# Two attentions and an MLP in one kernel: VectorE's order at a slot's head, inverse sums by transfer, and the order around the last attention

## The chip, the cores and the metric

The kernel runs on 1 core of one Trainium2 chip. Its time is the device time of one launch in microseconds (us). Three runs of the kernel before took 950.59, 950.79 and 953.49 us; their median is 950.79 us.

## What is computed

The input is 16 samples of 256 tokens with 256 features (x), a context y of the same shape, and the weights; all is float32. A sample goes through three attentions of 16 heads (16 features each) and an MLP. Cut to what matters:

```python
x = rmsnorm(x + softmax(rmsnorm(x) Wq . rmsnorm(y) Wk) rmsnorm(y) Wv Wo)   # layer 0: cross attention
h = ln(x);  x = x + attn(q=rope(h wq), k=rope(h wk), v=h wv, causal) wo    # layer 1: self attention
h = ln(x);  x = x + attn(q=rope(h wq), k=rope(y wk), v=y wv) wo            # layer 2: cross attention
h = ln(x);  out = x + gelu(h fc1) fc2                                      # MLP, 256 -> 1024 -> 256
```

Softmax is taken without subtracting a maximum. The sum of the exponentials comes out of the values' matmul as a seventeenth column of ones, and a record of all sums (`seen`) is looked at at the end: if one is too large, a second version of the layers runs. With these inputs it doesn't.

## The kernel before

There are 48 attentions (16 samples, 3 layers). `ORDER` (L31) gives their order by layer; attention i is run in slot i of the loop from L862 on. The order of every engine's instructions is the order of the code, since the whole is under a manual schedule (L845): nothing is reordered, and an instruction that waits holds up all that follow on its engine. DMAs are issued by SyncE's queue (SP), also in this order.

An attention has heads in two halves t and keys in two halves kc. A slot has four blocks (n = 0 to 3); with the causal mask it has three. In each block TensorE does the scores of the block (`scores`, L476, into a pair of two-bank PSUM tiles, tag S), the values of the block before (`value`, L515, into a one-bank tile, tag A, of which there is only one), and one dense product (L294 or L307, into a tag d, three of them). ScalarE turns scores into exponentials (L487) into `pt`, and for the causal attention GpSimd zeroes the part above the diagonal (L494). The values of an attention's last block come in block 0 of the next slot.

Around slot i, other attentions are at other stages:
- attention i + 2: its statistics (`stats`: squares at L246 for layer 0, batch-norm statistics at L256 and L257 else), its normalization (`norm`, L263), its transposes (`turn`, L274), and for layer 0 the query's scales that go through memory (`send`, `receive`: rq, L368 to L379);
- attention i + 1: q, k and v products, with rotation on VectorE (L406 to L435) and the values' bias (L456);
- attention i - 1: its last values; the inverse of its sums (`invert`, L549);
- attention i - 2: the multiplication by the inverse (`divide`, L564) and the output product (`project`, L572);
- attention i - 3, if of layer 0: `finish` (L581).

The way of the sums: ScalarE copies the values out of PSUM (L529); a DMA takes the rows of sums to DRAM (`hop`, L530) and one back in a form with 128 partitions (`sums`, L539), while eight DMAs bring the values into `oT` (L544). `invert` takes the reciprocal on VectorE (L554), adds the sums to `seen` on GpSimd (L555), sends the inverses to DRAM (L556), and one DMA of 8 rows brings them to every sixteenth partition of `first` (L560). `divide` spreads each to 16 partitions by a shuffle on VectorE (L566, into `inv`) and multiplies (L570).

VectorE's order in block 0 of a slot is: finish (i - 3), stats (i + 2), divide (i - 2), norm (i + 2), then the rotation of q (i + 1). For a causal slot with nothing to finish, stats come ahead of the scores; with something to finish, norm comes in block 1.

The MLP takes two samples at a time (`Mlp`, eight of them) and does each of its two products as seven products of a fast scheme (`up` 1, 5, 6, 2, 7, 3, 4, L711, and `down` with the same numbers, L772), with `mix` and `sum_a` making the sums that the scheme needs on VectorE. A result in PSUM is copied by ScalarE (`keep_sum`) or added by VectorE (`add_sum`); ScalarE does the gelu (L707). The first MLP's statistics, normalization and transposes are placed in the last two slots (L932 to L940), and after them L942 to L952 interleave the last attention's end with the first MLP's upward products. From L953 on, MLP g's downward products follow MLP g + 1's upward ones.

Of the kernel before, what the change touches and what calls it, by code (L numbers as in the profile page):

```python
# [42 lines left out]
FIRST = [i // HD * HD for i in range(32)]  # L43
# [3 lines left out]
def xattn_kernel(  # L47
# [99 lines left out]
    firsts = []  # L147
    for i in range(2):
        first = ctile([P, KC, S], f"first_{i}")
        nc.gpsimd.memset(first, 0.0)  # L150
        firsts.append(first)
# [13 lines left out]
    for i in range(2):  # L165
        pads.append([ctile([P, 32], f"pad{i}_{j}") for j in range(2)])
        nc.gpsimd.memset(pads[i][0], 0.0)

    idle = dense_ps()
    for n in range(2):  # L170
        nc.tensor.matmul(
            idle, lhsT=ident, rhs=firsts[0].rearrange("p t s -> p (t s)"), start=True, stop=True
        )
# [141 lines left out]
    class Att:  # L315
# [189 lines left out]
        def value(self, t, kc):  # L505
# [15 lines left out]
            if final:  # L521
                if t == 0:
                    self.av_sb = work.tile([P, KC, 2, S], F32, tag="av", name="av")
                    self.sums = work.tile([P, 2, 2 * H], F32, tag="sums", name="sums")
                    self.oT = work.tile([P, KC, S], F32, tag="oT", name="oT")

                    self.hop = dram.tile([2, KC, 8, S], F32, tag="hop", name="hop")
                av = self.av_sb[:, t]
                nc.scalar.copy(av, self.av)  # L529
                nc.sync.dma_start(  # L530
                    out=self.hop[0, t].rearrange("(r i) q -> r (i q)", i=2),
                    in_=av[HD:P:32].rearrange("r i q -> r (i q)"),
                )
                if t == 1:

                    for n in range(8):
                        r, i = n // 2, n % 2
                        if n == 3:
                            nc.sync.dma_start(  # L539
                                out=self.sums[:, 0], in_=self.hop[0].rearrange(  # L540
                                    "t g (a b) -> (t g a) b", b=2 * H
                                ),
                            )
                        nc.sync.dma_start(  # L544
                            out=self.oT[32 * r + HD * i : 32 * r + HD * i + HD],
                            in_=self.av_sb[32 * r : 32 * r + HD, :, i],
                        )

        def invert(self):  # L549

            sums = self.sums
            if self.layer == 0:
                nc.vector.tensor_scalar(sums[:, 0], sums[:, 0], 1e-30, None, ALU.max)
            nc.vector.reciprocal(sums[:, 1], sums[:, 0])  # L554
            nc.gpsimd.tensor_tensor(seen, seen, sums, ALU.add)  # L555
# [3 lines left out]
            self.first = firsts[self.i % 2]  # L559
            nc.sync.dma_start(  # L560
                out=self.first[0:P:HD], in_=self.hop[1].rearrange("t g q -> g t q")
            )

        def divide(self):  # L564
            inv = work.tile([P, KC, S], F32, tag="inv", name="inv", bufs=1)
            nc.vector.stream_shuffle(  # L566
                inv.rearrange("p t s -> p (t s)"),
                self.first.rearrange("p t s -> p (t s)"), FIRST,
            )
            nc.vector.tensor_tensor(self.oT, self.oT, inv, ALU.mult)  # L570
# [67 lines left out]
    class Mlp:  # L638
        def __init__(self, g, pool):
            self.g, self.pool = g, pool  # L640
            self.xs = [rows_of(2 * g + i) for i in range(2)]
# [4 lines left out]
        def norm(self):  # L646
            self.xns = [ln_apply(x, *st, self.pool) for x, st in zip(self.xs, self.st)]
            for x in self.xs:
                add_bias(x, R_FC2)

        def turn(self):
            self.hT = self.pool.tile([P, KC, 2, S], F32, tag="qm", name="hT3")
            for i, xn in enumerate(self.xns):
# [7 lines left out]
                nc.scalar.copy(self.hT[:, :, i, :], ps.rearrange("p (k s) -> p k s", s=S))  # L661

        def mix(self):

            b = self.hT
            self.ts = self.pool.tile([P, 4, S], F32, tag="av", name="ts")
            t1, t2, t3, t4 = (self.ts[:, i] for i in range(4))
# [14 lines left out]
        def half(self, i, j):  # L682

            if i == 0:
# [17 lines left out]
        def gelu(self, i, j, banks=None):  # L702
# [7 lines left out]

        def up(self, n):  # L711
            b, ts = self.hT, self.ts
            if n == 1:
                self.a = {}
# [3 lines left out]
                self.keep_sum(0, 0, self.X)  # L718
            elif n == 5:
                self.Z = psS.tile([P, 2, 512], F32, tag="S", name="upZ")  # L720
                self.Z = [self.Z[:, i] for i in range(2)]
                self.up_product(5, self.Z, up_s[0], ts[:, 0], True)
                self.keep_sum(1, 1, self.Z)
            elif n == 6:
                self.up_product(6, self.X, up_s[1], ts[:, 1], False)
                self.keep_sum(1, 0, self.X)
            elif n == 2:
                w = [dense_ps() for _ in range(2)]
                self.up_product(2, w, up_a(0, 1), b[:, 1, 0], True)
                self.add_sum(0, 0, w)  # L730
                self.gelu(0, 0)
            elif n == 7:
                self.up_product(7, self.X, up_a(1, 0), ts[:, 2], False)
                self.add_sum(1, 1, self.X)
                self.gelu(1, 1)
            elif n == 3:
                self.up_product(3, self.Z, up_s[2], b[:, 1, 1], False)
                self.add_sum(1, 0, self.Z)
                self.gelu(1, 0)
            elif n == 4:  # L740
                self.up_product(4, self.X, up_a(1, 1), ts[:, 3], False)
                self.a[0, 1] = self.half(0, 1)
                self.gelu(0, 1, self.X)

        def sum_a(self, n):

            if n == 1:
                self.s = {1: self.half(1, 2), 2: self.half(1, 3), 3: self.a[1, 0]}
# [23 lines left out]
        def down(self, n):  # L772
# [20 lines left out]
            if n == 1:  # L793
# [3 lines left out]
                self.X = bank(psA, "A")  # L797
# [47 lines left out]
    with tc.manual_schedule():  # L845
# [16 lines left out]
        for i in range(N_ATT):  # L862
# [7 lines left out]
            finishing = i >= 3 and att(i - 3).layer == 0  # L870
            for n in range(len(a.blocks)):
# [8 lines left out]
                if n == 0:  # L880
                    if i == 0:
                        a.v()
                        do(1, "spread")
# [529 lines left out]
```

## Time and profile before

| | us |
|---|---|
| median of three runs | 950.79 |
| the profiled execution | 953.16 |
| its span on the core | 951.43 |
| TensorE busy in it | 936.1 |
| VectorE busy | 666.0 |
| ScalarE busy | 571.9 |
| GpSimd busy | 294.6 |

The profile is that of one execution. PE is TensorE, DVE VectorE, ACT ScalarE, POOL GpSimd, SPq SyncE's queue. A row of the timeline has its start and its length in us, the engine, the line of the kernel, the operation, output<-input, shape and count; what stands in square brackets is how long the engine was idle just before and what ended that. A row of the list of waits has who waited, for whom, and then the total in us, how often, and the longest. A group of matmuls is counted busy from its first to its last, also if one in its middle waits. Float32 matmuls appear as two instructions each.

### The profile page before, as it was taken

The page shows a single profiled execution, that of the slowest core. Times are in us where ns is not written, and L with a number is a line of the kernel's source. Part 1 is how long each engine was busy: PE and PEld are TensorE (multiplying, and loading weights), DVE is VectorE, ACT ScalarE, POOL GpSimd, SP SyncE. Part 2 cuts the span into 40 slices and gives each one's busy share as a digit, 9 for nine tenths or more (in the row PEclk, how much of TensorE's full clock was granted, in tenths as well). Part 3 has the DMA queues.
Part 4 walks back from the last instruction along what each step waited for, and adds up shares of the span by engine and source line. Part 5 has one row for each costly group of instructions (what it writes and reads, how often), then busy time and mean ns, then how long its engine had stood idle before and what let it go on. Part 6 is the DMA issues. An engine that isn't in the chain of part 4 may idle for free.

```text
span 951.4 us, 30022 instructions
## 1 busy us (share of the span) xinstructions
PE 936.1 (98%) x12374; PEld 551.6 (58%) x12374; DVE 666.0 (70%) x1483; ACT 571.9 (60%) x821; POOL 294.6 (31%) x502
## 2 busy tenths in 40 slices
PE   8999999999999999999999999999999899999997
PEld 4444455445454545455454445445445699999997
DVE  4347768877776797677866768787776776667653
ACT  4666666766666766666766676666676634444440
POOL 4213454334334344144242423334112211222200
PEclk9999999999999999999999999999999999999999
DMA  9531221202121122110222101010101000000001
GB/s 316 171 97 29 78 71 32 71 18 79 25 70 28 42 54 73 24 33 19 72 71 74 32 22 27 19 29 21 26 21 26 13 24 23 13 12 23 23 24 47
DMA packets 66089, 46.96 MB, mean 49 GB/s; under 512 B 25364, under 2 KB 65044, under 8 KB 65944
## 3 DMA queue, kind: packets, MB, share of 16 engines
q1 hardware_dynamic: 64712, 43.89, 16.8%
q8 instruction: 100, 1.64, 0.7%
q10 hardware_dynamic: 1232, 1.07, 0.4%
q14 instruction: 45, 0.37, 0.1%
HBM read 26.54 MB, written 5.79 MB: 34 GB/s over the span
## 4 chain that ended last, share of the span: by engine, by line
PE 88%; DVE 5%; DMA 3%; POOL 1%; ACT 1%; issue 1%; SPq 0%; DVEq 0%; POOLq 0%
PE S L476 18%; PE A L515 17%; PE d L294 16%; PE d L307 15%; PE A L762 6%; PE upX L676 6%; PE downZ L762 3%; PE upZ L676 3%; PE d L274 2%; PE d L762 2%; PE d L676 1%; DMA hop<-av 1%; DVE a L410 1%; PE d L657 1%; DVE u L410 1%
## 5 line engine op out<-in xcount | busy, mean ns | idle before, releaser
L487 ACT ACTIVATE pt<-S 128x1024 f32<-128x1024 f32 x224 | 217.4, 1022 | 114.3 <-PE S L476 114.3
L476 PE MATMUL S<-qm,kT 32*128 32x512 f32 (+1 forms) x1536 | 202.9, 600 | 2.1 <-DVE kT L435 1.0
L515 PE MATMUL A<-pt,va 128*32 128x256 f32 (+1 forms) x3072 | 193.0, 367 | 1.3 <-POOL pt L494 0.8
L515 PEld LDWEIGHTS A<-pt,va 128*32 128x32 f32 x3072 | 80.5, 109 | 158.5 <-issue 95.4
L487 ACT ACTIVATE pt<-S,sy 128x1024 f32<-128x1024 f32 x128 | 135.7, 1111 | 46.1 <-PE S L476 44.0
L555 POOL TENSOR_TENSOR seen<-seen,sums 128x64 f32<-128x64 f32 x48 | 15.4, 320 | 280.4 <-DVE sums L554 185.8
L476 PEld LDWEIGHTS S<-qm,kT 32*128 32x128 f32 x1536 | 62.4, 183 | 68.5 <-issue 25.4
L494 POOL TENSOR_SCALAR_AFFINE_SELECT pt<-pt 128x512 f32<-128x512 f32 x128 | 88.5, 713 | 27.4 <-ACT pt L487 27.3
L283 POOL TENSOR_TENSOR cur<-cur,bias 128x512 f32<-128x512 f32 x48 | 65.3, 1365 | 58.9 <-DVE xn L263 58.9
L402 ACT ACTIVATE a<-d,qk_bias 128x256 f32<-128x256 f32 x128 | 53.8, 471 | 38.5 <-PE d L294 33.4
L294 PE MATMUL d<-hT,sa 128*32 128x256 f32 x1024 | 63.1, 379 | 0.0
L238 POOL TENSOR_SCALAR r_ln<-bmv 128x2 f32<-128x2 f32 x48 | 12.6, 261 | 153.3 <-DVE bmv L257 152.6
L529 ACT COPY av<-A 128x512 f32<-128x512 f32 x96 | 56.6, 590 | 3.5 <-PE A L515 3.2
L410 DVE TENSOR_TENSOR u<-u,turn 128x512 f32<-128x512 f32 x64 | 53.5, 836 | 0.0
L410 DVE TENSOR_TENSOR a<-a,turn 128x512 f32<-128x512 f32 x64 | 50.2, 784 | 2.2
L263 DVE TENSOR_SCALAR xn<-cur,bmv,r_ln 128x256 f32<-128x256 f32 x96 | 51.1, 579 | 0.8 <-POOL r_ln L239 0.6
L707 ACT ACTIVATE g<-g,fb 128x256 f32<-128x256 f32 x96 | 40.9, 497 | 15.4 <-DVE g L700 15.4
L579 DVE TENSOR_TENSOR cur<-d,cur 128x512 f32<-128x512 f32 x32 | 21.7, 679 | 38.8 <-PE d L307 38.7
L406 DVE STREAM_SHUFFLE u<-a 128x512 f32<-128x512 f32 x64 | 47.7, 746 | 0.0
L294 PEld LDWEIGHTS d<-hT,sa 128*32 128x32 f32 x1024 | 34.3, 110 | 22.1
L695 ACT COPY g<-upX 128x512 f32<-128x512 f32 x32 | 17.2, 589 | 46.8 <-issue 39.0
L757 DVE TENSOR_TENSOR g<-g,g 128x512 f32<-128x512 f32 x64 | 40.7, 681 | 0.0
(142 smaller groups left out, 1568.1 us busy)
## 6 DMA issues: line engine op xcount, KB each, us to landing
oT<-av SPq DMA_DIRECT2D x384, 32.0 KB
cur<-in_x SPq DMA_DIRECT2D x16, 256.0 KB
xT<-in_xt SPq DMA_DIRECT2D x16, 256.0 KB
yT<-in_yt SPq DMA_DIRECT2D x16, 256.0 KB
y<-in_y SPq DMA_DIRECT2D x16, 256.0 KB
out<-res SPq DMA_DIRECT2D x15, 256.0 KB
fc<-in_fc SPq DMA_DIRECT2D x2, 1024.0 KB
rq<-rq_hop SPq DMA_DIRECT2D x14, 128.0 KB
```

The costliest lines, as they stand in the source:

```text
L283: nc.gpsimd.tensor_tensor(t, t, bias_sb[:, row : row + D].unsqueeze(1).to_broadcast([P, NC, D]), ALU.add)
L294: nc.tensor.matmul(ps[j : j + 32, t * S : (t + 1) * S], lhsT=w[:, k, at + t * P + j : at + t * P + j + 32], rhs=src[:, k, :], start=(k == ...
L307: nc.tensor.matmul(ps[j : j + 32, c * D : (c + 1) * D], lhsT=src[:, k, c * P + j : c * P + j + 32], rhs=w[:, k, at : at + D], start=(k == ...
L402: nc.scalar.activation(a[:, t], ps[:, t], AF.Identity, bias=bias[:, t : t + 1])
L410: nc.vector.tensor_tensor(t, t, table.unsqueeze(1).to_broadcast([P, KC, S]), ALU.mult)
L476: nc.tensor.matmul(ps[:, j, 2 * m * u : 2 * m * (u + 1)] .rearrange("p (i s) -> p i s", i=2), lhsT=self.kT[r, t, kc * P : (kc + 1) * P], r ...
L487: nc.scalar.activation(pt[:, :, :w], ps[:, :, :w], AF.Exp, scale=scale)
L494: nc.gpsimd.affine_select(out=diag, in_=diag, compare_op=ALU.is_ge, fill=0.0, base=0, pattern=[[0, 2], [0, 2], [1, P]], channel_multiplier=-1,
L515: nc.tensor.matmul(self.av[32 * r : 32 * r + 32, i, q0:S], lhsT=self.va[:, kc, 8 * t + 2 * r + i, :], rhs=pts[r // 2][:, r % 2, i * m : (i ...
L529: nc.scalar.copy(av, self.av)
L676: nc.tensor.matmul(banks[c // 2][:, (c % 2) * S : (c % 2 + 1) * S], lhsT=a[:, c * P : (c + 1) * P], rhs=b, start=(first and c % 2 == 0), s ...
L762: nc.tensor.matmul(ps[:, c, :], lhsT=a[f // 2][:, f % 2, c * P : (c + 1) * P], rhs=b[:, f, :], start=(first and c == 0 and f == 0), stop=True,
```

## The change

Six things are changed:

1. The copy of attention i - 1's last values is split off (`take`, `end`) and done by VectorE in block 0 of slot i, after the statistics, unless these belong to the sample that `finish` has just written (`follows`); then it stands ahead of finish. Norm (i + 2) now precedes divide (i - 2). The first half's copy stays on ScalarE.
2. In place of the 8-row DMA and the shuffle, two DMAs read each inverse row 16 times and write all 128 partitions of `inv`, which now has two buffers. The two `first` tiles go; a tile of zeros takes their place in the two matmuls at the start.
3. The addition to `seen` moves from `invert` to `divide`, a slot later.
4. `invert` precedes `v` in the block before the last.
5. Around the last attention: the first MLP's statistics and normalization move to slots 45 and 46, the second's to 46 and 47; their transposes, the output product of attention 45 and the first MLP's product 2 are placed between the last slot's blocks; VectorE copies both transposes; `up` accepts products 1 and 2 in either order, and the gelu's order is written out by hand (`ups`).
6. For the last MLP, three of the four `sum_a` are done during the MLP before it, into other buffers, and the PSUM bank of its downward products comes from the tag S instead of A.

The diff, cut to its core:

```diff
-                av = self.av_sb[:, t]
-                nc.scalar.copy(av, self.av)
+                self.take(t, nc.scalar.copy)
+        def take(self, t, copy):
+            av = self.av_sb[:, t]
+            copy(av, self.av)
+            nc.sync.dma_start(out=self.hop[0, t]..., in_=av[HD:P:32]...)
+        def end(self, copy=nc.vector.tensor_copy):
+            self.take(1, copy)
+            for n in range(8):
...
             nc.vector.reciprocal(sums[:, 1], sums[:, 0])
-            nc.gpsimd.tensor_tensor(seen, seen, sums, ALU.add)
             nc.sync.dma_start(out=self.hop[1]..., in_=sums[:, 1])
-            self.first = firsts[self.i % 2]
-            nc.sync.dma_start(
-                out=self.first[0:P:HD], in_=self.hop[1].rearrange("t g q -> g t q")
-            )
+            self.inv = work.tile([P, KC, S], F32, tag="inv", name="inv")
+            for t in range(KC):
+                nc.sync.dma_start(
+                    out=self.inv[:, t],
+                    in_=self.hop[1, t].unsqueeze(1).to_broadcast([8, HD, S]),
+                )
         def divide(self):
-            inv = work.tile([P, KC, S], F32, tag="inv", name="inv", bufs=1)
-            nc.vector.stream_shuffle(inv..., self.first..., FIRST)
-            nc.vector.tensor_tensor(self.oT, self.oT, inv, ALU.mult)
+            nc.gpsimd.tensor_tensor(seen, seen, self.sums, ALU.add)
+            nc.vector.tensor_tensor(self.oT, self.oT, self.inv, ALU.mult)
...
+            follows = (
+                finishing and i + 2 < N_ATT
+                and att(i + 2).layer == 1 and att(i + 2).b == att(i - 3).b
+            )
...
                 if n == 0:
+                    if not follows and (finishing or not a.causal):
+                        do(i + 2, "stats")
+                    do(i - 1, "end")
                     do(i - 3, "finish")
-                    if finishing or not a.causal:
+                    if follows:
                         do(i + 2, "stats")
-                    do(i - 2, "divide")
                     if not finishing:
                         do(i + 2, "norm")
+                    if i == N_ATT - 3:
+                        mlps[0].stats()
+                    if i == N_ATT - 2:
+                        mlps[0].norm()
+                    do(i - 2, "divide")
+                    if i == N_ATT - 1:
+                        mlps[0].turn(nc.vector.tensor_copy)
+                        mlps[0].keep()
                     do(i + 1, "q")
                 elif n == 1:
...
+                    if i == N_ATT - 1:
+                        do(i - 2, "project")
+                        mlps[1].norm()
                 if n == final - 1:
+                    do(i - 1, "invert")
                     do(i + 1, "v")
-                    do(i - 1, "invert")
                     do(i + 2, "send")
+                    if i == N_ATT - 2:
+                        mlps[1].stats()
+                    if i == N_ATT - 1:
+                        mlps[0].up(2)
+                        mlps[0].mix("hT")
                 if n == final:
-                    do(i - 2, "project")
+                    if i == N_ATT - 1:
+                        mlps[1].turn(nc.vector.tensor_copy)
+                    else:
+                        do(i - 2, "project")
...
         last.values(-1)
+        last.end(nc.scalar.copy)
+        mlps[0].up(1)
         do(N_ATT - 2, "divide")
-        for n in (1, 5, 6, 2):
-            mlps[0].up(n)
+        mlps[0].ups(5, 6, (0, 0))
         do(N_ATT - 2, "project")
+        mlps[1].mix()
+        mlps[1].keep()
         last.invert()
-        for n in (7, 3, 4):
-            mlps[0].up(n)
-        mlps[1].turn()
-        mlps[1].mix()
+        mlps[0].ups(7, (1, 1), 3, 4, (0, 1), (1, 0))
...
+            if g == 0:
+                ahead.ups(2, 1)
...
+            final = g == B // 2 - 2
+            if final:
+                ahead.sum_a(1, ("qm", "av"))
             this.down(5)
+            if final:
+                ahead.sum_a(2)
...
-                self.X = bank(psA, "A")
+                if last:
+                    self.X = psS.tile([P, 2, 512], F32, tag="S", name="downX")
+                    self.X = self.X[:, 0, : NC * H2].rearrange("p (c d) -> p c d", d=H2)
+                else:
+                    self.X = bank(psA, "A")
```

In `ups` a tuple stands for the gelu of that quarter, a number for a product.

## The prediction

> **What bounds the kernel now.** I read the page's busy times first, then TensorE's own timeline from end to end, taking the distance from the start of one group of matmuls to the next, and last the list of waits.
>
> ```profile
> span 951.4 us, 30022 instructions
> ...
> PE 936.1 (98%) x12374; PEld 551.6 (58%) x12374; DVE 666.0 (70%) x1483; ACT 571.9 (60%) x821; POOL 294.6 (31%) x502
> ...
> PEclk9999999999999999999999999999999999999999
> ```
>
> TensorE is the bound at a full granted clock, and the change gives it the same matmuls; only their order near the end differs. So nothing is gained from shorter work on VectorE, ScalarE or GpSimd as such. What can be gained is time in which TensorE stands still or crawls, and 951.4 - 936.1 = 15.3 us understates it, since a group that waits in its middle counts as busy. I therefore use start-to-start distances. Undisturbed, scores to values take 1.07 us, values to a dense product 0.88, a dense product to the next scores 1.84: 3.80 a block. By that pace a slot without causal mask lasts 15.19 us (0.59 more with a transpose, 0.44 more after a causal slot), a causal slot 13.30. Most of the 47 slots before the last one have these lengths to 0.05 us. The excess lies in four places.
>
> (1) Slots. Over their own nominal length are slot 5 by 0.62, slot 6 by 0.98, 22 by 0.10, 29 by 1.00, 34 by 0.29, 39 by 0.48, 40 by 1.08, 41 by 0.83, 43 by 0.26: 5.6 us together. Slots 40 and 41 show both kinds:
>
> ```profile
> 625.83 0.66 PE L274 MATMUL d<-ident,xn 128*128 128x128 f32 x4
> 626.65 0.69 DVE L435 TENSOR_TENSOR kT<-a,u 128x512 f32<-128x512 f32 x1
> 627.49 1.14 PE L476 MATMUL S<-qm,kT 32*128 32x512 f32 x8 [1.01 <-DVE kT L435]
> 627.86 0.34 DVE L554 RECIPROCAL sums<-sums 128x32 f32<-128x32 f32 x1
> 628.29 0.32 POOL L555 TENSOR_TENSOR seen<-seen,sums 128x64 f32<-128x64 f32 x1 [5.77 <-DVE sums L554]
> 628.56 2.13 PE L515 MATMUL A<-pt,va 128*32 128x128 f32 x30
> 628.56 1.23 POOL L494 TENSOR_SCALAR_AFFINE_SELECT pt<-pt 128x512 f32<-128x512 f32 x2
> 630.52 0.39 PE L515 MATMUL A<-pt,va 128*32 128x256 f32 x2
> ```
>
> VectorE was late with the keys, so the scores began 1.0 us late. And GpSimd had stood still until the reciprocal, because the record of sums (L555) is ahead of the causal mask (L494) in its queue; the last two of 32 value matmuls came 0.6 us late. The list of waits gives the size of that block and of VectorE's own at a slot's head:
>
> ```profile
> POOL seen L555 <- DVE sums L554: 185.8, 34, 9.7
> ...
> DVE inv L566 <- DMA first<-hop: 34.7, 21, 3.6
> ```
>
> (2) The last attention and the first MLP, 721.1 to 767.1:
>
> ```profile
> 722.17 1.07 PE L515 MATMUL A<-pt,va 128*32 128x256 f32 x16
> 723.41 2.04 PE L476 MATMUL S<-qm,kT 32*128 32x512 f32 x8 [0.17 <-ACT pt L487]
> 725.38 1.07 PE L515 MATMUL A<-pt,va 128*32 128x256 f32 x16
> ...
> 739.68 1.89 PE L676 MATMUL d<-hT,fc 128*128 128x256 f32 x8
> 742.86 1.93 PE L307 MATMUL d<-cao,oT 128*32 128x256 f32 x32 [1.29 <-issue]
> ...
> 750.01 1.04 PE L657 MATMUL d<-ident,xn 128*128 128x128 f32 x8
> 752.88 1.99 PE L676 MATMUL upX<-hT,fc 128*128 128x256 f32 x8 [1.84 <-ACT hT L661]
> ```
>
> With nothing to project between blocks, scores overtake the exponentials: 0.24 + 0.90 (1.97 instead of 1.07) + 0.26. The projection at 742.86 comes 1.36 late (3.18 against 1.82), because its input was multiplied only at 741.6 to 742.8. The upward product at 752.88 comes 1.85 late (2.87 against 1.02), because ScalarE copies the transposed input behind eleven activations. Sum 4.6 us.
>
> (3) The entry to the last MLP:
>
> ```profile
> 930.97 1.95 PE L762 MATMUL A<-down_t,g 128*128 128x128 f32 x16
> 933.53 2.02 PE L762 MATMUL A<-fc,g 128*128 128x128 f32 x16 [0.61 <-DVE res L779]
> ```
>
> 2.56 instead of 1.78, as both groups use the one bank A; then 0.21 and 0.10 while VectorE does six sums at once. 1.1 us. (4) The first 30 us and the tail after the last VectorE operation at 947.0: about 6 us that no edit touches.
>
> **The change, part by part.**
>
> *Record of sums moved from invert to divide.* The 48 additions of 320 ns stay, but now stand at a slot's head, where their input is a slot old. The mask behind them no longer waits for a reciprocal. This covers slots 6, 22, 29, 34, 39, 41, 43: 3.9 us. What is late next is the exponential that the mask reads, and that is on time.
>
> *Head of a slot.* Statistics, copy of the last values, finish, norm, divide stand in this order, so VectorE works where it waited for the inverse. In slot 40 it sat idle 3.2 us until 617.64, then did shuffle, multiply and norm and reached the query's shuffle at 620.01. Now norm goes first (values end at 615.1, copy to 615.8, norm to 616.9) and only the multiply waits. The inverse must then be there by about 619 for the stall of 1.0 to go.
>
> *Copy of the values on VectorE.* 47 copies leave ScalarE (590 ns each; nothing waits for that there). VectorE's nearest row, 128x512 with one input from PSUM (L579), has 679 ns: 47 x 0.68 = 32 us more, against 48 x (745 + 14) ns = 36 us of shuffle and mask load less. Even. The bounds are 0.59 and 0.69; both end even. The copy waits for TensorE, and behind it stand finish, norm, divide and the query's evacuation. Values end about 2.0 us into the slot, the copy 2.9, and the next values need the bank at 4.87: 2 us of cover. It is about 1 us earlier than ScalarE's, which came behind two exponentials (288.03 in the slot that begins at 284.70), and so are the sums behind it.
>
> *Repeated inverse by transfer.* One DMA of 8 rows becomes two that write 128 partitions with 1 KB each. SyncE pays one more issue of 0.64 us per slot; in its queue the query scales (rq) and the next sample's loads stand behind that. The small DMA's data came 1.93 us after its issue (615.71 to 617.64). Packets cost 0.168 x 16 x 951.4 / 64712 = 40 ns at 678 bytes, so an estimated 60 ns at 1 KB; 256 packets over 16 engines are 1.0 us, so 2.9 us after the first issue. The Trainium skill (DMA: Bandwidth & Descriptors, "Why a DMA increments its semaphore by 16 and not by 1") speaks against that: the number of engines is the largest up to 16 that divides the slowest dimension of both patterns, and here the source begins with 8 heads, so 8 engines and 1.9 us: 3.8 us after issue. No row here tells the two apart. I take 3.8. Against 1.93 + 0.76 for transfer and shuffle this is 1.1 us later; the reciprocal, now ahead of the values' bias addition (680 ns), starts 0.7 earlier. In most slots TensorE doesn't feel it: the product reads oT ten microseconds after the head, and keys have 1.2 to 7 us of margin (end of the keys' last addition to the scores that read them). Keys with less than 0.8 us are those of slots 5, 22, 29, 39, 41, 43. I leave slot 5, where the stall is the late rq, unrecovered, count half of slot 40's and charge 0.9 us for new waits. Slots: 3.9 + 0.5 - 0.9 = 3.5, bounds 5.6 and -1.
>
> *Filled last attention.* The same groups in the order scores, values, transposes / scores, values, projection / scores, values, product 2 / scores, values, transposes / values, products. A filler takes 1.02 to 1.87, so scores begin 3.1 us or more after the last ones and find their bank free. Inputs: the first MLP's rows are normalized a slot earlier (2.3 us of VectorE where it idled 3.1 us at 707.6); transposes are copied by VectorE (4 x 0.68), so none waits behind activations; attention 46's inverse has all of slot 47. The last values may wait 0.3 for the exponential, and products 6 and 7 follow VectorE closely. 4.6 - 0.5 = 4.1 us.
>
> *Last MLP.* The first bank comes from the S pair, which products no longer need; six sums of 0.64 move into the MLP before, where VectorE was 12.65 of 23.8 us busy. 1.1 us. The idle start matmuls read another zero tile: nothing.
>
> Sum: 4.1 + 1.1 + 3.5 = 8.7. The profiled execution took 953.16, of which the span is 951.43; after, 942.7 of span and 944.5 for the execution. The median of the runs shown is 2.4 lower than that execution. If those 2.4 lie outside the span, the median after is 942.1; if they are slot stalls the other runs did not have, it stays 944.5. I put 943.0.
>
> **Rivals.**
>
> *All of it goes* (0.12): no new wait at all, 4.6 + 1.1 + 5.6 = 11.3, 939.5. For it: most slots have over 1.2 us margin.
>
> *The slots' stalls change place* (0.20): the mask runs on time, but an inverse or rq that is 1 us later delays six tight slots by as much as is won, and the last attention gives 3 of its 4.6: about 4, 946.8. For it: the 8 engines, and six margins under 0.8 us. Against it: the norm now precedes the wait.
>
> *Slower* (0.05): the copy holds the values' only PSUM bank. Where two samples' squares stand ahead of it (13 slots), VectorE enters late and TensorE waits for the bank. The 2 us cover must be overrun by 8.7 / 13 = 0.67 us in each to cancel everything; by 0.95 us it is 954. Against it: in eight of these slots the squares end by 2.4 us after the head, when the copy's input has only just come.
>
> The forecast itself has 0.63.
>
> **How the numbers follow.** Low end: 939.5 less the 0.2 by which runs differ, 939.3. High end: just past the second rival, 947.6. Measurement can tell about 0.3%, 2.9 us, from no change. Faster by that means under 947.9: the first case, all of it, and most of the second rival, 0.89. Same 0.06, slower 0.05.
>
> **What would show it.** Right: no wait of GpSimd's record for a reciprocal; value groups after causal slots unbroken; the first downward product of the first MLP 4 us or more earlier after slot 47's head than 46.0; 1.78 between the last two MLPs; slots 29, 39 and 41 at 16.22. Wrong: waits of TensorE for the copy of the values, VectorE waiting longer for the inverse than 34.7 us with keys late behind it, or product 6 waiting for VectorE.

## The result, and the profile after

The changed kernel takes 946.16 us (median of six runs, 945.57 to 947.51); the kernel before, run beside it, 952.05 (six runs, 950.59 to 953.49). The ratio is 0.9942, with a 95% interval of 0.9929 to 0.9954: 5.9 us faster. The profiled execution took 945.63 us, 943.8 of it span.

From the page of the changed kernel, the span and the first busy times:

```profile
span 943.8 us, 29943 instructions
...
PE 931.4 (99%) x12374; PEld 550.1 (58%) x12374; DVE 656.8 (70%) x1438; ACT 546.8 (58%) x770; POOL 297.6 (32%) x501
```

The same 12374 matmuls, 7.6 us less span. Start-to-start distances of TensorE's groups, as in the prediction, say where they went. "Excess" is what slots last beyond their undisturbed length (13.30 and 15.19 us with the prediction's additions; the 0.59 for a transpose is now left out in slots that transpose nothing).

| profiled execution, us | before | after | difference |
|---|---|---|---|
| start of slot 0 | 10.89 | 11.06 | +0.17 |
| excess of slots 0 to 3 | 2.50 | 2.70 | +0.20 |
| excess of slots 4 to 9 | 2.19 | 4.30 | +2.11 |
| excess of slots 10 to 46 | 5.35 | 0.07 | -5.28 |
| head of slot 47 to first downward product | 46.04 | 42.31 | -3.73 |
| first to last downward product | 177.48 | 176.34 | -1.14 |
| rest | 6.8 | 6.8 | 0 |

So the last attention, the last MLP and all late slots gave what they had, and some of it was lost again in slots 4 to 9. TensorE's timeline of the changed kernel around slot 41's head:

```profile
625.82 1.14 PE L472 MATMUL S<-qm,kT 32*128 32x512 f32 x8
...
626.89 1.51 PE L511 MATMUL A<-pt,va 128*32 128x128 f32 x32
```

The scores wait for no keys (1.01 before), and the 32 value matmuls of the causal slot are one unbroken group of 1.51 (2.13 and a rest of 0.39 before). The last attention and the entry to the last MLP, in the same view:

```profile
720.37 1.09 PE L657 MATMUL d<-ident,xn 128*128 128x128 f32 x8
721.40 1.26 PE L472 MATMUL S<-qm,kT 32*128 32x512 f32 x8
...
737.08 1.89 PE L681 MATMUL upX<-ts,up_s 128*128 128x256 f32 x8
738.90 1.93 PE L303 MATMUL d<-cao,oT 128*32 128x256 f32 x32
...
926.23 1.95 PE L779 MATMUL downX<-fc,g 128*128 128x128 f32 x16
928.01 1.95 PE L779 MATMUL downZ<-down_t,g 128*128 128x128 f32 x16
```

A filler stands between blocks; the projection follows the upward product by 1.82 (3.18 before); and the groups of the last MLP are 1.78 apart (2.56 before). The list of waits shows what is new:

```profile
DVE qm L417 <- DMA rq<-rq_hop: 36.1, 12, 4.8
...
POOL seen L566 <- DVE sums L554: 19.0, 2, 12.5
...
PE A L511 <- DVE av L528: 2.5, 2, 1.6
```

GpSimd's record waited for a reciprocal 34 times before; the two waits that are left stand in and behind the last slot. VectorE's waits for the inverse are down to 8.0 us in the same list (34.7 before). But TensorE now waits for VectorE's copy of the values, in slots 4 and 6: the mechanism of the prediction's "slower" rival. And VectorE waits longer for the queries' scales rq: 36.1 us, 23.8 before.

### The profile page after: what moved, and what is told of

Read it like the earlier page. It is cut to its first block, busy times and chain, and to the rows that moved or that the text cites. A ratio compares the mean times of both kernels' runs of the same rounds, so it can differ in the third digit from the quotient of the medians.

```text
span 943.8 us, 29943 instructions
## 1 busy us (share of the span) xinstructions
PE 931.4 (99%) x12374; PEld 550.1 (58%) x12374; DVE 656.8 (70%) x1438; ACT 546.8 (58%) x770; POOL 297.6 (32%) x501
## 3 DMA queue, kind: packets, MB, share of 16 engines
q8 instruction: 100, 1.64, 0.7%
q10 hardware_dynamic: 1232, 1.07, 0.4%
## 4 chain that ended last, share of the span: by engine, by line
PE 87%; DMA 6%; DVE 4%; SPq 2%; issue 1%; POOL 0%; ACT 0%; ACTq 0%; DVEq 0%
PE S L472 17%; PE A L511 16%; PE d L303 15%; PE d L290 15%; PE upX L681 6%; PE A L779 5%; PE downZ L779 3%; PE upZ L681 3%; PE d L270 2%; PE d L779 2%; PE d L681 1%; DMA hop<-sums 1%; DMA sums<-hop 1%; DMA hop<-av 1%; DMA rq_hop<-pad 1%; PE d L657 1%
## 5 line engine op out<-in xcount | busy, mean ns | idle before, releaser
L511 PE MATMUL A<-pt,va 128*32 128x256 f32 (+1 forms) x3072 | 188.9, 367 | 2.5 <-DVE av L528 2.5
L567 DVE TENSOR_TENSOR oT<-oT,inv 128x512 f32<-128x512 f32 x48 | 41.5, 864 | 30.5 <-DMA hop<-av 8.5
L290 PE MATMUL d<-hT,sa 128*32 128x256 f32 x1024 | 61.2, 379 | 0.0
L406 DVE TENSOR_TENSOR a<-a,turn 128x512 f32<-128x512 f32 x64 | 48.1, 752 | 2.2
L417 DVE SCALAR_TENSOR_TENSOR qm<-d,vec,rq 128x512 f32<-128x512 f32 x32 | 22.5, 746 | 38.8 <-DMA rq<-rq_hop 36.1
L406 DVE TENSOR_TENSOR u<-u,turn 128x512 f32<-128x512 f32 x64 | 49.2, 768 | 0.0
L528 DVE COPY av<-A 128x512 f32<-128x512 f32 x47 | 32.2, 684 | 21.8 <-PE A L511 21.8
L234 POOL TENSOR_SCALAR r_o<-ms_o 128x2 f32<-128x2 f32 x16 | 5.1, 322 | 128.9 <-DVE sq L242 117.0
```

What stands on the lines that cost most here:

```text
L290: nc.tensor.matmul(ps[j : j + 32, t * S : (t + 1) * S], lhsT=w[:, k, at + t * P + j : at + t * P + j + 32], rhs=src[:, k, :], start=(k == ...
L406: nc.vector.tensor_tensor(t, t, table.unsqueeze(1).to_broadcast([P, KC, S]), ALU.mult)
L511: nc.tensor.matmul(self.av[32 * r : 32 * r + 32, i, q0:S], lhsT=self.va[:, kc, 8 * t + 2 * r + i, :], rhs=pts[r // 2][:, r % 2, i * m : (i ...
```

## The experiments

The times of before beside these runs were 952.22, 951.98 and 952.15 us. The table has the excess from each kernel's one profiled execution, which for e1, e2 and e3 took 1.9 to 3.6 us more than the median, so that their columns are at the upper end. The last column, the time that the inverses of slot 40 take out to memory, is explained under code loading, below.

| kernel | median us | ratio, 95% interval | slots 4-9 | slots 10-46 | head 47 to down | slot 40: excess (way of the inverses to memory) |
|---|---|---|---|---|---|---|
| before | 952.05 | 1 | 2.19 | 5.35 | 46.04 | 1.08 (3.07) |
| after | 946.16 | 0.9929-0.9954 | 4.30 | 0.07 | 42.31 | 0.01 (1.46) |
| e1_v_first | 948.10 | 0.9951-0.9977 | 4.80 | 3.48 | 42.31 | 1.65 (3.45) |
| e2_copy_first | 949.88 | 0.9965-0.9990 | 6.99 | 5.22 | 42.31 | 1.65 (2.99) |
| e3_both | 953.30 | 1.0005-1.0026 | 6.63 | 7.59 | 42.49 | 1.66 (3.09) |
| e4_record | 945.18 | 0.9917-0.9952 | 2.58 | 1.32 | 42.32 | 0.00 (1.46) |
| e10_record_only | 949.43 | 0.9959-0.9979 | 0.21 | 1.56 | 46.45 | 1.45 (2.61) |
| e5_shuffle | 942.50 | 0.9885-0.9918 | 0.00 | 0.18 | 42.76 | 0.05 (1.42) |
| e11_end_act | 947.87 | 0.9928-0.9961 | 6.01 | 0.12 | 42.31 | 0.00 (1.47) |
| f1_spare_rows | 944.63 | 0.9904-0.9935 | 4.24 | 0.12 | 42.77 | 0.00 (1.48) |
| f2_spare_repeated | 945.22 | 0.9912-0.9947 | 3.15 | 0.06 | 42.77 | 0.00 (1.46) |
| f3_shuffle_but_last | 942.82 | 0.9887-0.9920 | 1.12 | 0.20 | 42.32 | 0.05 (1.42) |
| e6_old_last | 947.92 | 0.9945-0.9975 | 3.00 | 0.02 | 44.87 | 0.00 (1.46) |

**First theory: VectorE's order at the head is what makes slots 4 and 6 wait.** In the changed kernel, VectorE stood at the inverse's sums until 75.48 us with the values' bias behind them; then came four squares, then the copy, 1.59 us late for TensorE. Three kernels change that order, one takes the record's move back.

e1: the values' bias ahead of the inverse, as before.

```diff
-                    do(i - 1, "invert")
                     do(i + 1, "v")
+                    do(i - 1, "invert")
```

> The changed kernel with one thing put back: the values' bias (v) stands ahead of invert again. Theory (VectorE's own queue makes the new waits of slots 4 to 7): in slot 3 the bias and all behind it no longer wait 3.3 us for the sums, so the copy of slot 4 is about 0.9 us earlier and its wait of 1.6 us shrinks to about 0.7; the same in slot 6; the reciprocals come 0.7 us later, which the late slots bear. About 945.2 us against 946.2 for the changed kernel. Rival (the larger inverse transfers make those waits): no change, 946.2.

e2: the copy always ahead of the statistics.

```diff
-                    if not follows and (finishing or not a.causal):
-                        do(i + 2, "stats")
                     do(i - 1, "end")
+                    if not follows and (finishing or not a.causal):
+                        do(i + 2, "stats")
```

> The changed kernel with the copy of the last values ahead of the statistics in every slot. Theory: the waits of TensorE for that copy in slots 4 and 6 (1.6 and 0.9 us) go, while the squares come up to 0.7 us later, which can lengthen the two waits for the query scales by as much: 944.2 us, between 943.5 and 945.5. Rival (transfers): the waits stay, 946.2. Second rival: statistics behind the copy make norm and keys late in the slots with 0.4 us of margin, 947 or more.

e3: both.

> Both edits together: bias ahead of invert, copy ahead of the statistics. Theory: the two gains overlap, since both free the same copy; 943.9 us, at most 0.5 below the copy alone. Rival (transfers): 946.2.

All three are slower than the changed kernel, by 1.9 (the intervals just touch), 3.7 and 7.1 us, and the more of the cure, the worse. Slot 4 of e1 loses 0.56 in place of 1.67, as the theory said, but slots 35 and 40 now stall (1.49 and 1.65). In e2, with the copy first, no matmul of slots 4 and 6 waits for the copy any more, and yet they lose 2.19 and 3.17: in slot 6 a product waits 1.88 us for the values' bias. The theory fell. Slot 40 of e1, VectorE, TensorE and SyncE's queue:

```profile
614.72 0.33 SPq L555 DMA_DIRECT2D hop<-sums  x1
...
618.17 1.30 SPq L560 DMA_DIRECT2D inv<-hop  x2
...
621.79 0.86 DVE L567 TENSOR_TENSOR oT<-oT,inv 128x512 f32<-128x512 f32 x1 [2.92 <-DMA inv<-hop]
...
630.28 1.14 PE L472 MATMUL S<-qm,kT 32*128 32x512 f32 x8 [1.58 <-DVE kT L431]
```

The inverses' way out to memory took 3.45 us (614.72 to 618.17, where the next transfer may be issued), against 1.46 in the changed kernel; the multiplication, the rotation behind it and the keys are late in turn.

e4: the record of sums put back where it was, all else as changed.

```diff
             nc.vector.reciprocal(sums[:, 1], sums[:, 0])
+            nc.gpsimd.tensor_tensor(seen, seen, sums, ALU.add)
...
         def divide(self):
-            nc.gpsimd.tensor_tensor(seen, seen, self.sums, ALU.add)
```

> The changed kernel with the record of sums back in invert, right behind the reciprocal. Theory: the causal mask waits for reciprocals again, and the slots after a causal one (29, 34, 39, 41, 43) lose what they had lost before less the 0.7 us by which the reciprocal is now earlier: 2.5 us in all, 948.7. Rival (the gain of those slots comes from VectorE's new order alone): no change, 946.2.

945.18: the time is no longer than with the move. Two slots, 6 and 34, show the old block, and no other does; slot 34:

```profile
521.98 0.32 POOL L555 TENSOR_TENSOR seen<-seen,sums 128x64 f32<-128x64 f32 x1 [5.58 <-DVE sums L554]
...
523.09 1.43 PE L511 MATMUL A<-pt,va 128*32 128x256 f32 x14 [0.55 <-POOL pt L490]
```

They lose 1.40 and 1.33 us in this execution. In slots 29, 39, 41 and 43 the reciprocal is 0.4 to 1.1 us earlier against the slot's head than in the kernel before, and there before the mask is due. That comes from its place ahead of the bias: in e1, where the bias is first again, it comes 0.2 to 0.4 us behind the head, about as late as before the change.

e10 is the counterpart: the kernel before, with the record moved and nothing else.

```diff
-            nc.gpsimd.tensor_tensor(seen, seen, sums, ALU.add)
...
         def divide(self):
             ...
+            nc.gpsimd.tensor_tensor(seen, seen, self.sums, ALU.add)
```

> The kernel before with one step of the change alone: the addition into the record of sums goes from `invert` to `divide`, one slot later. All else is as before. The prediction's account (the record holds the mask additions on GpSimd back, 3.9 us in the late slots): about 3.5 to 3.9 us faster than before, near 948.4. The rival, formed after the record put back into the changed kernel cost nothing (945.18 us): it is VectorE's order that brings the reciprocals forward, and the record only stood behind them; then GpSimd is freed here as well, the mask additions no longer wait for the reciprocal, and this alone also recovers most of the 3.9 us. A third reading, that the stalls of slots 22, 29, 39, 40, 41 and 43 come from VectorE's own lateness and not from the record: no more than 1 us faster, 951 to 952.

949.43, 2.6 us faster (by the interval 2.0 to 3.9); in the trace the slots from 10 on fall from 5.35 to 1.56, of which 1.45 is slot 40. So the record's move alone removes these waits, and the rest of the change alone removes all of them but two; the gains don't add.

**Second theory: the repeated transfers of the inverse cost slots 4 to 9.** e5 takes back part 2 of the change alone.

```diff
-            self.inv = work.tile([P, KC, S], F32, tag="inv", name="inv")
-            for t in range(KC):
-                nc.sync.dma_start(
-                    out=self.inv[:, t],
-                    in_=self.hop[1, t].unsqueeze(1).to_broadcast([8, HD, S]),
-                )
+            self.first = firsts[self.i % 2]
+            nc.sync.dma_start(
+                out=self.first[0:P:HD], in_=self.hop[1].rearrange("t g q -> g t q")
+            )
         def divide(self):
+            nc.vector.stream_shuffle(inv..., self.first..., FIRST)
```

> The changed kernel with the inverse brought as before: one transfer of the first row of each head and a shuffle on VectorE, in place of two repeated transfers. Theory: the inverse of the shuffled way is there after 1.93 + 0.76 = 2.7 us instead of the 3.72 to 3.78 us that the repeated transfers take, so that no slot is later, and the late keys of slot 7 (0.62) may go; VectorE's 0.76 us a slot lies in its idle time: 945.5 to 946.2, no different from the changed kernel. Rival: VectorE at a slot's head is what bounds the slots 4 to 7 and others, and 0.76 us more ahead of the queries and keys costs 0.1 to 0.7 us in some ten slots: 948 to 950.

Both expectations missed, on the good side: 942.50 us, 3.7 less than the changed kernel, and its interval (0.9885 to 0.9918) lies clear of that one's. No slot from 4 on has an excess over 0.1. Slots 3 and 4 of the changed kernel, SyncE's queue, VectorE and TensorE:

```profile
61.76 1.29 SPq L560 DMA_DIRECT2D inv<-hop  x2
...
65.68 0.32 SPq L375 DMA_DIRECT2D rq<-rq_hop  x1
66.05 0.43 SPq L93 DMA_DIRECT2D cur<-in_x  x1
...
70.14 1.41 DVE L417 SCALAR_TENSOR_TENSOR qm<-d,vec,rq 128x512 f32<-128x512 f32 x2 [3.91 <-DMA rq<-rq_hop]
...
75.48 0.18 DVE L553 TENSOR_SCALAR sums<-sums 128x32 f32<-128x32 f32 x1 [3.29 <-DMA sums<-hop]
...
80.81 0.69 DVE L528 COPY av<-A 128x512 f32<-128x512 f32 x1
...
81.64 1.07 PE L511 MATMUL A<-pt,va 128*32 128x256 f32 x16 [1.59 <-DVE av L528]
```

and the same steps with the shuffled inverse:

```profile
61.62 0.63 SPq L564 DMA_DIRECT2D first<-hop  x1
...
64.53 0.32 SPq L380 DMA_DIRECT2D rq<-rq_hop  x1
64.91 1.17 SPq L94 DMA_DIRECT2D cur<-in_x  x1
...
67.74 1.41 DVE L422 SCALAR_TENSOR_TENSOR qm<-d,vec,rq 128x512 f32<-128x512 f32 x2 [1.33 <-DMA rq<-rq_hop]
...
72.95 0.18 DVE L558 TENSOR_SCALAR sums<-sums 128x32 f32<-128x32 f32 x1 [3.17 <-DMA sums<-hop]
```

From the first inverse transfer to the queries scaled by rq it is 8.38 us there and 6.12 here. The second transfer's issue holds the queue; rq, the next sample's four loads and the sums stand behind it; rq comes 2.3 us later, the sums 2.4, and VectorE reaches the copy too late. Of rq's 2.3 us, 1.0 is there when its own transfer is issued (3.92 us behind the first inverse transfer, against 2.91). The other 1.3 comes after that: 4.46 us from its issue to its use, against 3.20. There the two differ in the first load behind rq, whose issue takes 1.17 us with the shuffle and 0.43 in the changed kernel, so that the loads follow rq more closely. The thirteen kernels have 58 transfers of rq with loads behind them for which VectorE waited. Where that first issue took 1.17 us or more, rq was used 2.9 to 3.3 us after its issue (7 cases); where it took under 0.5, over 4.0 us (44 of 47). That loads close behind it slow rq down is an inference: no kernel moved them alone.

The distance from the first inverse transfer to rq's use is 6.05 to 6.27 us in the four kernels with one transfer (before, e10, e5, f3) and 7.27 to 8.84 in the seven with the repeated ones. The list of waits of e5 has, for the 36.1 above:

```profile
DVE qm L422 <- DMA rq<-rq_hop: 13.1, 8, 3.4
```

e11 asks whether the copy itself is at fault: it goes back to ScalarE at its new place.

```diff
-                    do(i - 1, "end")
+                    if i > 0:
+                        att(i - 1).end(nc.scalar.copy)
```

> The changed kernel with the copy of the last values on ScalarE again, at its new place in the program, so that VectorE neither makes the copy nor holds the values' bank behind the squares of two samples. Theory: the waits for this copy in slots 4 (1.59 us) and 6 (0.90) go, and the time falls by about 2 us to 944.2. Rival: on ScalarE the copy stands behind the exponentials of the new slot's first scores, 1.5 to 2 us later than on VectorE where that is free, the sums and the inverse come that much later in every slot, the keys behind the multiplication by the inverse have margins of only 0.15 to 0.7 us in many slots, and the time rises to 949 or more.

TensorE no longer waits for the copy, and yet slots 4 to 9 lose 6.01: the same lateness ends in waits for the query (0.63), the values' bias (1.47) and the keys (0.96). The theory's 944.2 is wrong; the rival's place, the late slots, is wrong too (0.12). At 947.87 (no different from the changed kernel by the intervals) the copy's engine is not the cause.

f1 and f2 are to separate the issue from the bytes. To the shuffled version they add a transfer that nothing reads, behind the real one: f1 the same 8 rows (16 KB), f2 one repeated transfer of 128 KB. Both use one `first` buffer.

```diff
+            nc.sync.dma_start(
+                out=spare[0:P:HD], in_=self.hop[1].rearrange("t g q -> g t q")
+            )
```

```diff
+            nc.sync.dma_start(
+                out=spare[:, 0], in_=self.hop[1, 0].unsqueeze(1).to_broadcast([8, HD, S])
+            )
```

> The shuffled version of the changed kernel (942.5 us) with a second transfer of the same 8 rows behind the first, 16 KB into a buffer that nothing reads (all slots use one buffer for the first rows instead of two). The shuffled version is 3.7 us faster than the changed kernel because slots 4 to 7 don't wait: there the queries' inverse roots went out 1 us earlier behind the inverse on SP's queue. Theory A, the issue time: the second repeated transfer holds SP's queue some 0.65 us and moves all that stands behind it (the roots, the next samples' loads, the sums). Then this spare transfer of nearly the same issue time brings a good part of the waits back: 944 to 946.5. Theory B, the bytes: 256 KB written by half the DMA engines delay what is queued behind them in those engines; then 16 KB more cost nothing: 942 to 943.

> As the run with the spare 8 rows, but the spare transfer is one repeated transfer of 128 KB (8 rows, each to 16 partitions), which nothing reads. Theory A, the issue time: the same as with the spare 8 rows, within 1 us (944 to 946.5). Theory B, the bytes: half of the changed kernel's loss, 943.5 to 945.5, and at least 1 us more than with the spare 8 rows.

944.63 and 945.22, where nothing added gives 942.50: theory A's range for both, and no 1 us between them. rq's distance is 7.78 and 7.11. One more transfer brings back 2.1 to 2.7 of the 3.7 us; what the bytes add (0.6 between the two) can't be told from zero. The times alone don't settle it, since both intervals touch that of e5 (up to 0.9918). rq's distances, outside the 6.05 to 6.27 of one transfer, speak for the issue, but only in part: rq's own issue is 0.65 and 0.74 us later than in e5, and the rest is again a longer way from its issue to its use (4.23 and 3.46 us against 3.20). So the repeated transfers cost 3.7 us; how much of it is the second issue and how much the closer loads stays open. f1's profiled execution (947.32) was the longest of its six, so its 4.24 is at the upper end.

f3 is put together from this: the shuffle for all attentions but the last two.

```diff
+            if self.i >= N_ATT - 2:
...
+                return
```

> The version that is put together from the findings: the changed kernel with the shuffled inverse in all attentions but the last two, which keep the repeated transfers; in these last two no roots or loads follow on SP's queue, and VectorE is in the way of the mixing sums of the last stage (from the last slot's head to the first down product 42.76 us with the shuffle, 42.31 with the transfers). Theory: 0.45 us less than the shuffled version, 942.0 to 942.3. Rival: the 0.45 us came from the shuffle's place in the last slot only by chance, and nothing is gained: 942.4 to 943.

942.82, the same as e5. The trace has the 0.44 us in its place (42.32 against 42.76), but slots 5 and 6 cost 1.1 in that execution; a gain isn't shown. Both beat the changed kernel and the one before (by 9.5 and 9.3 us).

**The last attention alone.** e6 takes back its filling and the placing of the first MLPs' steps.

```diff
-                    if i == N_ATT - 1:
-                        do(i - 2, "project")
-                        mlps[1].norm()
...
-                    if i == N_ATT - 1:
-                        mlps[0].up(2)
-                        mlps[0].mix("hT")
...
+                if i == N_ATT - 1 and n == 2:
+                    mlps[0].turn()
+                    mlps[0].mix()
```

> The changed kernel with the last attention's filling and the last MLP's new order taken back (where the MLPs' steps stand, and the order of their products); slots 4 to 45 are those of the changed kernel. Theory: from the last slot's head to the first down product 46.0 us again instead of 42.3, and the MLPs without the early sums 0.9 to 1.1 us longer: 946.16 + 3.7 + 0.9 = 950.8, between 950 and 951.5. Rival: with the late slots no longer waiting, the old last attention is itself shorter than it was in the kernel before (its wait was for work that came late), and less than 2.5 us is lost: under 948.7.

The kernel kept the last MLP's early sums and bank, which its expectation counted as undone; the theory's figure for what was undone is 946.16 + 3.7 = 949.9. It took 947.92, and the trace shows 44.87 in place of 46.04: the rival is right that the old order is itself shorter now, but not as to why. One of the old waits had gone without the filling, as the timeline of e6 shows:

```profile
736.33 1.89 PE L681 MATMUL d<-hT,fc 128*128 128x256 f32 x8
...
737.57 0.68 DVE L567 TENSOR_TENSOR oT<-oT,inv 128x512 f32<-128x512 f32 x1
...
738.35 1.93 PE L303 MATMUL d<-cao,oT 128*32 128x256 f32 x32
```

and of the kernel before:

```profile
740.79 0.72 DVE L566 STREAM_SHUFFLE inv<-first 128x512 f32<-128x512 f32 x1
...
741.55 1.21 DVE L570 TENSOR_TENSOR oT<-oT,inv 128x512 f32<-128x512 f32 x1
```

2.02 between the two products, 3.18 before. The statistics and the normalization ahead of this multiplication stand where they stood, to 0.2 us. What is gone is the shuffle (0.72), and the multiplication itself is shorter (0.68 against 1.21, for a reason that no run shows); it ends 20.49 us after slot 47's head, 21.66 before. That is the gain of the repeated transfers in this place. The other two waits (scores on exponentials, and 2.87 to the upward product behind ScalarE's copies) are back. So the filling is worth 44.87 - 42.31 = 2.56 us beside the transfers (1.8 by the medians, whose intervals overlap), and 46.04 - 42.76 = 3.28 beside the shuffle (e5).

**The transfers by themselves.** e8 leaves out all of the model's computation and runs the transfers in a row, each with a multiplication that needs it; it ran once.

> The transfers by themselves; all of the model's computation is left out. Eight times in a row, each followed by a dependent multiplication on VectorE: the transfer of 8 rows (as before the change), the two repeated transfers of 128 KB each from 8 rows (as in the change), the same two with 16 rows as source, and one load of 256 KB by rows. If the repeated transfers are long by the number of engines that take part (8 of 16): from the first issue to the multiplication some 1.9 us for 8 rows, 3.7 to 3.8 for the pair from 8 rows, about 2.9 for the pair from 16 rows. Rival, the issue time of two transfers on one queue and the latency of each set it: the pair from 16 rows takes as long as that from 8, within 0.2 us.

| from first issue to the multiplication, us | mean of 8 | range |
|---|---|---|
| 8 rows, 16 KB (four places) | 2.02 to 2.09 | 1.95 to 2.39 |
| two repeated, source of 8 rows | 3.49 | 3.40 to 3.53 |
| two repeated, source of 16 rows | 3.16 | 3.07 to 3.21 |
| 256 KB by rows | 2.73 | 2.53 to 2.89 |

Neither expectation holds as it stands: 16 rows are quicker, but by 0.33 us and not by 0.9.

## Why the prediction was right or wrong, point by point

It said faster, with 943.0 and a range to 947.6; the time was 946.16. The span was forecast at 942.7 and was 943.8. That it came so near is in part luck: two errors of about 2 us, one in the late slots and one in slots 4 to 9, had opposite signs. Of the signs that it named, 1.78 between the last MLPs and 16.22 in slots 29, 39 and 41 came, and the value groups are unbroken; the last attention stayed just under its "4 us or more"; and one sign of being wrong came, the waits for the copy.

*Last attention* (4.1): 3.73, right in mechanism. But the filling is not all of it. In e6, with the repeated transfers and without the filling, 1.17 is won already, since the shuffle ahead of attention 46's multiplication is gone; the filling adds 2.56. The other way round, the filling with the shuffle (e5) gives 3.28 and the transfers 0.45 more. The prediction gave the repeated transfers nothing there.

*Last MLP* (1.1): 1.14.

*Record of sums* (3.9): by itself it gives 2.6 (2.0 to 3.9), and the cause is only half of it. e10 removes these waits by the record alone, e4 all but two of them without it. "The mask behind them no longer waits" is true, but the earlier reciprocal does mostly the same, so the change holds two remedies for one wait. The slots themselves were under-sized: 6, 22 and 34 had 1.57, 0.69 and 0.88 of excess and not 0.98, 0.10 and 0.29, since a transpose was counted in them that they don't have. With all of slot 40's stall this makes the gain of slots 10 to 46 5.28, where the prediction counted 3.5.

*Head of a slot* (half of slot 40's stall, 0.5): all of it went, 1.07. The step took the stall for VectorE's order alone; it comes and goes with the inverses' way out to memory (3.07 before, 1.46 after).

*Repeated inverse* (charged 0.9 for new waits): this is the step that failed in size. "SyncE pays one more issue of 0.64 us per slot; in its queue the query scales (rq) and the next sample's loads stand behind that" named the path; then it was priced by the keys' margins at the inverse, which held. What came late was rq and all behind it in slots 4 to 9. Their excess is 4.30, 2.1 us more than before and 4.3 more than with the shuffle in the profiled executions; by the medians the shuffle is 3.7 us faster. In place of 0.9 the new waits cost about 4. The prediction compared the arrival of the inverse with that of the shuffled one, not the queue's next entries. For that arrival 3.8 was estimated with the Trainium skill ("DMA: Bandwidth & Descriptors", section "Why a DMA increments its semaphore by 16 and not by 1": a source whose slowest dimension is 8 uses 8 of the 16 engines), against 2.9 from the packets' row. Measured in the kernel, from the first issue to the multiplication: 3.72 (94.10 to 97.82) and 3.78 (78.93 to 82.71). The value held; its working did not quite, since by e8 the number of rows is worth 0.33 us and not 0.9.

*Copy on VectorE* (even): right as to the load. The "slower" rival's wait did come, in slots 4 and 6 (1.59 and 0.90), but e11 shows it to be where the late rq surfaced, not a price of the copy. "The slots' stalls change place" (946.8) came nearest to the time, for a reason of its own kind: the late rq, not keys behind the inverse, and the last attention gave 3.73 and not 3.

*From the profiled execution to the median* (1.5 us taken off): wrong. Time outside the span is 1.7 to 1.8 us in both; runs differ inside it. The three runs shown had a low median (950.79; in later sets of 6 to 43 runs it was 951.98 to 952.22), and the changed kernel's median lies 0.5 above its profiled execution. With the span's 1.1 these 2.0 make up the miss of 3.2 us.

## What to carry to other kernels

Before a transfer is split in two or widened, list what stands behind it on its queue and price the delay of those, not only the arrival of its own data: here a second, wider transfer, with one more issue of 0.65 us, cost 3.7 us through scales and loads three steps away, while the shuffle that it saved (0.76 us a slot on VectorE) had cost TensorE time in the last slot alone (0.45 us). When an engine is late at one instruction, moving that instruction to another engine moves the wait; look for what came late in front of it. Where two edits of one change remove the same wait, undo each alone and do each alone, or their gains will be added twice.

## What the runs showed of the hardware

*Code loading meets small transfers.* The page lists DMAs that load instructions (queue q8: 100 transfers, 1.64 MB, so 16 KB each). The inverses' way out to memory in slot 40 of e1, in the DMA view of the 1.4 us after its issue at 614.72:

```profile
q8 instruction: 1, 0.02, 5.5%
```

The changed kernel has no q8 row in the same stretch (611.21 to 612.61). From the issue of this way out (16 KB) to that of the transfer that needs it, it is 1.40 to 2.0 us in 447 cases of the thirteen kernels and 2.0 to 3.65 in 177. Of the 177 long ones, 145 have a load of q8 begin in their first 1.4 us; of the 447 short ones 16. The place in the program doesn't explain it: in 25 of the 48 attentions the same transfer met such a load in some kernels and not in others, and took 2.77 us in the mean of 161 cases where it did, 1.70 in the 164 where it didn't. In the table's last column slot 40 stalls in exactly the five kernels where it was long (2.61 to 3.45), and in none with 1.42 to 1.48. In these five it also begins later against the slot's head (0.1 to 0.6 us before it, against 1.0 to 1.4), so a small shift both delays it and lets it meet the load; the two were not tried apart. That the load is the cause is an inference from this coincidence: no kernel moved the loads by themselves. It would explain the 2.4 to 3.1 us that e1 to e3, with small shifts of order, lost in slots 35 and 40; what they lost elsewhere stays unexplained.

*Runs of one kernel differ by several us inside the span*: it is 948.5 to 952.4 in eleven runs of before, at a granted clock of 0.998 to 1.0, and 945.4 to 953.4 in the 22 runs of e2, at 0.997 to 1.0. The thirteen kernels' traces differ in the start (slot 0 begins at 10.85 to 12.47 us) and in slots 4 to 9, where samples are loaded while rq and the sums are on their way.
